# Two FP4 feed-forward layers taken in steps between the pieces of attention, with another rounding and another silu

## The chip, the cores and the metric

The kernel runs on one NeuronCore of a Trainium2 chip, in one launch, in fp32. The metric is the time of the run on the device in microseconds (us). TensorE is called PE, VectorE DVE, ScalarE ACT, GpSimd POOL and SyncE SP, as the profile does; PEld is PE's loading of weights.

## The reference

Input x has 8 batches of 512 tokens of width 128. The block does, one after the other, each with a residual:

```python
x = x + 0.5 * ffn(layernorm(x))        # FP4 feed-forward
x = x + attn(layernorm(x))             # 16 heads of 64, softmax over 512 keys
x = x + 0.5 * ffn(layernorm(x))        # the same FP4 feed-forward again
x = x + 0.5 * moe(x); x = x + linear_attention(x); x = x + 0.5 * moe(x)
```

The FP4 feed-forward rounds both operands of each product, in blocks of 16 along the summed axis, to a grid times the block's scale:

```python
scale = max(max(|block|) / 6, 1e-12)
q = sign(b / scale) * nearest(|b / scale|, [0, .5, 1, 1.5, 2, 3, 4, 6]) * scale
h = silu(q(x) @ q(w_gate).T) * (q(x) @ q(w_up).T)      # 128 -> 352
y = q(h) @ q(w_down).T                                 # 352 -> 128
```

All is per token except attention, which mixes the 512 tokens of one batch. Batch 3's second feed-forward, for instance, needs only batch 3's attention.

## The kernel before

A tile of 512 tokens is one batch, held in SBUF as `xs[t]`, 128 rows by 4 chunks by 128. The program calls its stages in order: `ffn4(0)`, `attention()`, `ffn4(1)`, `moe(0)`, `linear_attention()`, `moe(1)`. Each engine has a queue of its own. Except where `manual_schedule` fixes PE's order as written, a scheduler sets the order in which the instructions stand in each queue; waits between engines are added from the data and from the buffers.

**Feed-forward (`ffn4`).** `hidden(t)` normalises a tile (`ln_stats` every four tiles, with a `Sqrt` on ACT; `ln_apply` on DVE), rounds it (`quantize`, lines 200 to 214: nine instructions, of which the last, L214, is on POOL and the others on DVE), transposes it (L254), and for each chunk of 128 tokens makes two products of 352 columns in two PSUM tiles (L264 `pg`, L265 `pu`), `Silu` on ACT (L267) and the product on DVE (L268). `down(t)` rounds the hidden layer (1408 columns), transposes it (L277), multiplies by `wdn` (L286) and adds to `xs[t]` (L293). Tile t+1's `hidden` is written ahead of tile t's `down`.

**Attention (`attention`).** It loops over 64 pairs of heads, g, eight for each batch. In iteration g PE does, in the order written: `scores` of chunks 0 and 1 (L360, `pS`), `project_q(g+1)` (`pq`, L332), `transposes(g-1, 2)` (L387, `pT`), `times_v(g-1, 0)` (L402, `po`), `transposes(g-1, 3)`, `project_k(g+1)` (`pk`, L338), `scores` of chunks 2 and 3, `spread(g-1)` (transposes of the inverse sums into `pr`, L181), `transposes(g, 0)`, `times_v(g-1, 1)`, `transposes(g, 1)`, `project_v(g+1)` (`pv`, L346). DVE takes the maxima (L369) and copies seven of eight `pT` (L392); ACT does Exp with the sums (L372) and copies q, k, v, one `pT` and `pr`. Every eighth iteration has `project_out` (`py`, L430), and `prepare` of the next batch (layer norm, transposes `xhT`).

**PSUM.** Attention's pools are `a_sc` (`pS`, two buffers of two banks), `a_pt` (`pT`, two) and `a_o` (`po`, one). The pool `misc` has `bufs=1` and lives through the whole program:

```python
misc = ctx.enter_context(tc.tile_pool(name="misc", bufs=1, space=PSUM))
```

`pq`, `pk`, `pv`, `pr`, `py` and `xhT` all use that one tile, so each waits until the one ahead has been read.

Of the kernel before, what the change touches and what calls it, by code (L numbers as in the profile page):

```python
# [15 lines left out]
P = 128  # L16
# [18 lines left out]
EXP_BITS = 0x7F800000  # L35
MAGIC = 1.5 * 2.0**22
TOWARD_ZERO = 1.0 - 2.0**-23


@with_exitstack  # L40
def macaron_kernel(
# [125 lines left out]

    def ln_apply(dst, xt, stats, i):
        mv, rstd = stats
        for c in range(NC):  # L170
            k = i * NC + c
            nc.vector.tensor_scalar(  # L172
                dst[:, c, :], xt[:, c, :], mv[:, k, 0:1], rstd[:, k : k + 1],
                ALU.subtract, ALU.mult,
            )
# [8 lines left out]
    def ln_transposed(dst, xt, stats, i):  # L184
        xh = norm.tile([P, NC, D], F32, name="xh", tag="xh")
        ln_apply(xh, xt, stats, i)
        ps = transpose4(xh, "xhT")
        nc.scalar.copy(dst, ps)


    def quantize(pool, src, tag, n):
# [4 lines left out]
        def blocks(t):  # L196
            return t.rearrange("p (n k) -> p n k", k=BLOCK)

        sc = pool.tile([P, nb], F32, name=f"{tag}_sc", tag=f"{tag}_sc")
        nc.vector.tensor_reduce(sc, blocks(src), AX.X, ALU.max, apply_absolute_value=True)  # L200
        nc.vector.tensor_scalar(sc, sc, 1.0 / 6.0, 1e-12, ALU.mult, ALU.max)
        rs = pool.tile([P, nb], F32, name=f"{tag}_rs", tag=f"{tag}_rs")
        nc.vector.reciprocal(rs, sc)
        xn = pool.tile([P, n], F32, name=f"{tag}_xn", tag=f"{tag}_xn")
        nc.vector.tensor_tensor(blocks(xn), blocks(src), rs[:, :, None].to_broadcast(bc), ALU.mult)
        mg = pool.tile([P, n], F32, name=f"{tag}_mg", tag=f"{tag}_mg")
        nc.vector.tensor_scalar(
            mg.bitcast(I32), xn.bitcast(I32), EXP_BITS, None, ALU.bitwise_and
        )
        nc.vector.tensor_scalar(mg, mg, 1.0, MAGIC, ALU.max, ALU.mult)  # L210
        nc.vector.scalar_tensor_tensor(xn, xn, TOWARD_ZERO, mg, ALU.mult, ALU.add)
        nc.vector.tensor_tensor(xn, xn, mg, ALU.subtract)
        xq = pool.tile([P, n], F32, name=f"{tag}_xq", tag=f"{tag}_xq")
        nc.gpsimd.tensor_tensor(blocks(xq), blocks(xn), sc[:, :, None].to_broadcast(bc), ALU.mult)  # L214
        return xq
# [23 lines left out]
    def ffn4(ph):  # L239
        with tc.tile_pool(name=f"f{ph}_sb", bufs=2) as sb, tc.tile_pool(  # L240
            name=f"f{ph}_gu", bufs=2, space=PSUM
        ) as ps_gu, tc.tile_pool(name=f"f{ph}_t", bufs=3, space=PSUM) as ps_t:
            stats = {}

            def hidden(t):

                if t % GT == 0:
                    stats[t // GT] = ln_stats(xs[t : t + GT])
                xh = norm.tile([P, NC, D], F32, name="xh", tag="xh")
                ln_apply(xh, xs[t], stats[t // GT], t % GT)  # L250
                xq = quantize(sb, xh.rearrange("p c d -> p (c d)"), "x4", NC * D)
                pst = ps_t.tile([P, TT], F32, name="xqT_ps", tag="t")
                for c in range(NC):
                    nc.tensor.transpose(  # L254
                        pst[:, c * P : (c + 1) * P], xq[:, c * D : (c + 1) * D], ident
                    )
                xqT = sb.tile([P, TT], F32, name="xqT", tag="xqT")
                nc.scalar.copy(xqT, pst)
                h = sb.tile([P, NC, FI], F32, name="h", tag="h")
                for c in range(NC):  # L260
                    pg = ps_gu.tile([P, FI], F32, name="pg", tag="pg")
                    pu = ps_gu.tile([P, FI], F32, name="pu", tag="pu")
                    lhsT = xqT[:, c * P : (c + 1) * P]
                    nc.tensor.matmul(pg, lhsT, wgu[:, 0, :], start=True, stop=True)  # L264
                    nc.tensor.matmul(pu, lhsT, wgu[:, 1, :], start=True, stop=True)  # L265
                    sg = sb.tile([P, FI], F32, name="sg", tag="sg")
                    nc.scalar.activation(sg, pg, AF.Silu)  # L267
                    nc.vector.tensor_tensor(h[:, c, :], sg, pu, ALU.mult)  # L268
                return h

            def down(t, h):
                hq = quantize(sb, h.rearrange("p c f -> p (c f)"), "h4", NC * FI)
                hqT = sb.tile([P, 3, TT], F32, name="hqT", tag="hqT")
                for r, (k0, kn) in enumerate(FK):
                    pst = ps_t.tile([P, TT], F32, name="hqT_ps", tag="t")
                    for c in range(NC):
                        nc.tensor.transpose(  # L277
                            pst[:kn, c * P : (c + 1) * P],
                            hq[:, c * FI + k0 : c * FI + k0 + kn],
                            ident,  # L280
                        )
                    nc.scalar.copy(hqT[:kn, r, :], pst[:kn, :])
                py = ps_t.tile([P, NC, D], F32, name="py", tag="t")
                for c in range(NC):
                    for r, (k0, kn) in enumerate(FK):
                        nc.tensor.matmul(  # L286
                            py[:, c, :],
                            hqT[:kn, r, c * P : (c + 1) * P],
                            wdn[:kn, r, :],
                            start=(r == 0),  # L290
                            stop=(r == 2),
                        )
                nc.vector.scalar_tensor_tensor(xs[t], py, 0.5, xs[t], ALU.mult, ALU.add)  # L293

            h = hidden(0)
            for t in range(NB):
                ahead = hidden(t + 1) if t + 1 < NB else None
                down(t, h)
                h = ahead
# [4 lines left out]
    def attention():  # L304
        scale = DH**-0.5
        with tc.tile_pool(name="a_sb", bufs=2) as sb, tc.tile_pool(
# [9 lines left out]
            def prepare(b):  # L316
                if b % GT == 0:
                    stats[b // GT] = ln_stats(xs[b : b + GT])
                hTs[b] = sb.tile([P, TT], F32, name="hT", tag="hT")
                ln_transposed(hTs[b], xs[b], stats[b // GT], b % GT)  # L320

                nc.gpsimd.tensor_tensor(
                    xs[b], xs[b], bo_sb[:, None, :].to_broadcast([P, NC, D]), ALU.add
                )
                oTs[b] = sb.tile([P, NPAIR, TT], F32, name="oT", tag="oT")
# [96 lines left out]
            def finish(g):  # L422
                b, pr = divmod(g, NPAIR)
                nc.vector.tensor_tensor(oTs[b][:, pr, :], pos.pop(g), rs.pop(g), ALU.mult)
# [10 lines left out]

            prepare(0)
            project_q(0)
            project_k(0)
            project_v(0)

            pe_order = ExitStack()
            pe_order.enter_context(tc.manual_schedule(engines={mybir.EngineType.PE}))
            for g in range(NPT + 1):
# [8 lines left out]
                if old:  # L452
                    transposes(g - 1, 2)
                    times_v(g - 1, 0)
                    transposes(g - 1, 3)
                if nxt:
                    project_k(g + 1)
                if new:
                    scores(g, 2)
                    scores(g, 3)  # L460
# [6 lines left out]
                if old:  # L467
                    times_v(g - 1, 1)
                    finish(g - 1)
                if new:  # L470
                    transposes(g, 1)
# [475 lines left out]
```

## Time and profile before

| what | us |
|---|---|
| median of 3 runs (2442.45 to 2444.76) | 2443.05 |
| the profiled execution, own time | 2272.8 |
| its span, first to last instruction | 2271.1 |
| weights and first feed-forward, up to attention | 189.2 |
| attention | 1025.4 |
| second feed-forward | 154.9 |
| routing, experts, linear attention, experts | 901.6 |

The profile is of one execution, and all durations below are from it; it was 170 us shorter than the runs that were timed. A line number is that of the kernel before. Busy time of PE is modelled from the instruction and its successors, so PE that shows as busy is not PE at its peak; PEclk is the share of PE's full clock that was granted. A matrix product in fp32 shows as two records, a transpose as one.

### The profile page before, as it was taken

To read this page: it belongs to the slowest core of one execution; us is meant where nothing else is said; L and a number is where in the kernel's file an instruction comes from. 1 tells how busy PE (TensorE), PEld (TensorE's weight loads), DVE (VectorE), ACT (ScalarE), POOL (GpSimd) and SP (SyncE) were. 2 spreads that over 40 slices of the span, in tenths; PEclk is the share of its full clock that TensorE was granted. 3 is DMA by queue.
4 is the path that set the end of the run, shared out by engine and by line. 5 is a ranking of instruction groups with operands and counts; after the bars stand their busy time and mean duration, and the time that the engine had idled before them with its cause. 6 is when DMAs were issued, how large, how long until landed. Compare 5 with 4: busy or idle time off the path is not lost.

```text
span 2271.1 us, 31365 instructions
## 1 busy us (share of the span) xinstructions
PE 1869.2 (82%) x11321; PEld 1283.6 (57%) x11321; DVE 1509.5 (66%) x3392; ACT 946.5 (42%) x2439; POOL 467.3 (21%) x458
## 2 busy tenths in 40 slices
PE   2767999999999999999996755887439999859781
PEld 1544666665666566665664545654327777646560
DVE  8986756666575656666567994444379999745342
ACT  1324545555455545545451321232226767413230
POOL 1221000000000000000000220773332122227615
PEclk9888999999999999999998875797769999858885
DMA  6000000000000000000000001241100000013312
GB/s 175 1 0 1 1 1 1 1 1 1 1 1 1 1 1 1 1 1 1 1 1 1 1 0 37 56 93 48 48 18 1 1 1 1 20 35 74 85 58 65
DMA packets 57032, 47.61 MB, mean 21 GB/s; under 512 B 6512, under 2 KB 51760, under 8 KB 56880
## 3 DMA queue, kind: packets, MB, share of 16 engines
q1 hardware_dynamic: 46720, 26.16, 4.0%
q0 software_dynamic: 9216, 18.89, 3.8%
q8 instruction: 93, 1.52, 0.3%
q10 hardware_dynamic: 944, 0.54, 0.1%
q14 instruction: 59, 0.48, 0.1%
HBM read 28.80 MB, written 16.78 MB: 20 GB/s over the span
## 4 chain that ended last, share of the span: by engine, by line
PE 72%; DVE 14%; DMA 5%; issue 3%; POOL 3%; ACT 2%; POOLq 0%; DVEq 0%; ACTq 0%
PE pS L360 11%; PE pT L387 11%; PE po L402 10%; PE ph L690 5%; DMA yk<-yg,rows 4%; PE pym L714 3%; PE pq L332 3%; PE py L430 3%; PE pv L346 3%; PE pk L338 2%; PE ptok L629 2%; PE pm L855 2%; PE lpq L812 2%; PE lpo L874 2%; PE py L286 2%
## 5 line engine op out<-in xcount | busy, mean ns | idle before, releaser
L372 ACT ACTIVATE pe<-pS,nmax 128x512 f32<-128x512 f32 x512 | 348.7, 692 | 289.9 <-DVE nmax L369 216.3
L369 DVE TENSOR_REDUCE nmax<-pS 128x2 f32<-128x1024 f32 x256 | 302.0, 1218 | 131.6 <-PE pS L360 131.6
L392 DVE COPY aT<-pT 128x512 f32<-128x512 f32 x448 | 290.4, 684 | 97.5 <-PE pT L387 97.4
L387 PEld LDWEIGHTS pT<-ident,pe 128*128 128x128 f32 x2048 | 227.3, 141 | 86.6 <-issue 68.7
L387 PE MATMUL pT<-ident,pe 128*128 128x128 f32 x2048 | 273.1, 276 | 2.1 <-DVE aT L392 2.1
L360 PE MATMUL pS<-kT,qT 64*128 64x512 f32 x1024 | 256.4, 619 | 0.8 <-ACT pe L372 0.8
L402 PE MATMUL po<-aT,v 128*64 128x256 f32 x2048 | 249.6, 386 | 0.0
L414 POOL COPY wide<-rsum 128x512 f32<-128x512 f32 x64 | 39.3, 613 | 962.7 <-PE pT L387 903.8
L690 PE MATMUL ph<-wall,xgT 128*128 x320 | 166.3, 645 | 29.2 <-DVE g L696 21.7
L660 POOL DMA_INDIRECT xgs<-xg,toks x160 | 157.0, 981 | 157.7 <-DVE toks L634 109.5
L402 PEld LDWEIGHTS po<-aT,v 128*64 128x64 f32 x2048 | 136.2, 137 | 76.6 <-issue 21.3
L360 PEld LDWEIGHTS pS<-kT,qT 64*128 64x128 f32 x1024 | 88.6, 187 | 117.8 <-issue 109.4
L748 POOL DMA_INDIRECT yk<-yg,rows x128 | 120.9, 944 | 156.3 <-DMA yg<-ygs 111.0
L696 DVE TENSOR_TENSOR g<-g,ph 128x256 f32<-128x256 f32 x160 | 66.6, 419 | 112.3 <-ACT g L695 109.3
L695 ACT ACTIVATE g<-ph 128x256 f32<-128x256 f32 x160 | 60.9, 383 | 172.9 <-PE ph L690 172.9
L752 DVE SCALAR_TENSOR_TENSOR x<-yk,m,x 128x128 f32<-128x128 f32 x128 | 44.7, 353 | 118.6 <-DMA yk<-yg,rows 118.4
L806 POOL TENSOR_TENSOR y<-y,bout_sb 128x512 f32<-128x512 f32 x48 | 61.7, 1286 | 220.2 <-DVE xh L172 220.2
L372 ACT ACTIVATION_READ_ACCUMULATOR pe<-pS,nmax 128x1 f32 x512 | 105.8, 207 | 0.0
L690 PEld LDWEIGHTS ph<-wall,xgT 128*128 128x128 f32 x320 | 59.0, 207 | 79.9 <-issue 37.0
L277 PE MATMUL hqT_ps<-ident,h_xq 128*128 128x128 f32 (+1 forms) x192 | 35.1, 350 | 80.3 <-POOL h_xq L214 80.3
L798 PE MATMUL ph<-ident,xh 128*128 128x128 f32 x192 | 31.9, 295 | 72.6 <-DVE xh L172 72.5
L714 PE MATMUL pym<-wall,gT 128*128 x640 | 87.8, 296 | 1.4 <-DVE gT L707 1.4
(193 smaller groups left out, 3354.6 us busy)
## 6 DMA issues: line engine op xcount, KB each, us to landing
yg<-ygs SPq DMA_DIRECT2D x40, 256.0 KB, 2.4
xg<-mxh SPq DMA_DIRECT2D x16, 256.0 KB, 2.3
xgs<-xg,toks POOLq DMA_INDIRECT x160, 2.6
x<-in_x SPq DMA_DIRECT2D x8, 256.0 KB, 4.5
yk<-yg,rows POOLq DMA_INDIRECT x128, 2.5
out<-x SPq DMA_DIRECT2D x8, 256.0 KB, 2.5
wall<-in_w1T SPq DMA_DIRECT2D x1, 1024.0 KB, 9.2
wall<-in_w2T SPq DMA_DIRECT2D x1, 1024.0 KB, 11.5
```

The lines of the kernel that those rows point to most:

```text
L332: nc.tensor.matmul(ps, wq_sb[:, cols(g)], hTs[g // NPAIR], start=True, stop=True)
L346: nc.tensor.matmul(ps[:, c, :], hT[:, c * P : (c + 1) * P], wv_sb[:, cols(g)], start=True, stop=True,)
L360: nc.tensor.matmul(ps[:, j, :], qTs[g][rows, c * P : (c + 1) * P], kTs[g][rows, :], start=True, stop=True,)
L369: nc.vector.tensor_reduce(nmax, ps, AX.X, ALU.max, negate=True)
L372: nc.scalar.activation(pe[:, j, :], ps[:, j, :], AF.Exp, bias=nmax[:, j : j + 1], accum_out=sums[g][:, 2 * c + j : 2 * c + j + 1],)
L387: nc.tensor.transpose(ps[:, k, :], pe[:, j, k * P : (k + 1) * P], ident)
L392: nc.vector.tensor_copy(dst, ps)
L402: nc.tensor.matmul(pos[g][rows, half * 2 * P : (half + 1) * 2 * P], vs[g][:, k, rows], aT[:, j, k, :], start=(k == 0), stop=(k == NC - 1),)
L660: nc.gpsimd.indirect_dma_start(x[:, s, :], None, xg[:, :], bass.IndirectOffsetOnAxis(ap=toks[:, q * QS + s : q * QS + s + 1], axis=0),)
L690: nc.tensor.matmul(ph.rearrange("p a h -> p (a h)"), xTs[q][:, s, :], wall[:, bass.ds(at, 2 * HID)], start=True, stop=True,)
L714: nc.tensor.matmul(py[:, s, :], gs[q][:, s, k, :], wall[:, bass.ds(ats[q * QS + s] + (2 * HID + k * D), D)], start=(k == 0), stop=(k == NH ...
L748: nc.gpsimd.indirect_dma_start(yk, None, yg[:, :], bass.IndirectOffsetOnAxis(ap=rows[:, j, k : k + 1], axis=0),)
```

## The change

It touches three things.

**Where the feed-forward stands.** `ffn4` is gone. `feed_forward(t)` is a Python generator with 18 `yield`s; each step emits a part of the work of one tile. `ffn(0)` runs to its end ahead of attention. From then on `beside()` is called four times in each iteration, after `times_v(g-1, 0)`, between `scores` 2 and 3, after `finish(g-1)` and at the iteration's end, and emits one step of the tile at the head of a queue, and one of the next tile too for the next tile's first four steps (`AHEAD`). A tile's first feed-forward is queued two batches ahead of its attention, its second when `project_out` of its batch has been emitted; `ffn(7)` of the second layer runs after the loop. The PSUM tiles are attention's own: `xqT_ps` and `hqT_ps` share `pT`'s two banks, `pg` and `py` share `misc`. All of it is inside PE's manual order.

**The instructions of a tile.** The layer norm of these tiles (`tile_stats`, `tile_apply`, also used by attention's `prepare`) takes the inverse root from an integer guess on DVE and three Newton steps on POOL, and applies it on ACT. `quantize` works in place with the block's negative scale: DVE multiplies, ACT takes the magnitude times a factor (`Abs`), and DVE adds and subtracts a rounding step with the maximum taken in the same instruction, so 3 wide DVE instructions and one on ACT stand where there were 5 on DVE; the last product stays on POOL. Silu is made from tanh: `(tanh(g/2) + 1) * g * u`, twice its value, made good by 0.25 instead of 0.5 at the end. Gate and up are taken in halves of 176 columns, both in one PSUM bank, and the hidden layer is rounded two chunks at a time.

**Buffers.** `oT` has one buffer instead of two, and is taken at the batch's first `finish`.

The core of the diff (`stat` tiles' allocations and the removed lines of `ffn4` left out):

```diff
+    def tile_stats(xt):
...
+        nc.vector.tensor_scalar(v, mv[:, :, 1], EPS, None, ALU.add)
...
+        nc.vector.tensor_scalar(bits, v.bitcast(I32), 1, None, ALU.logical_shift_right)
+        nc.vector.tensor_scalar(rstd.bitcast(I32), bits, -1, RSQRT_GUESS, ALU.mult, ALU.add)
+        nc.gpsimd.tensor_scalar(v, v, -0.5, None, ALU.mult)
...
+        for _ in range(3):
+            nc.gpsimd.tensor_tensor(sq, rstd, rstd, ALU.mult)
+            nc.gpsimd.tensor_tensor(sq, sq, v, ALU.mult)
+            nc.gpsimd.tensor_scalar(sq, sq, 1.5, None, ALU.add)
+            nc.gpsimd.tensor_tensor(rstd, sq, rstd, ALU.mult)
...
+        nc.gpsimd.tensor_tensor(shift, mv[:, :, 0], rstd, ALU.mult)
+        nc.gpsimd.tensor_scalar(shift, shift, -1.0, None, ALU.mult)
+        return rstd, shift
+
+    def tile_apply(xt, stats):
...
+            nc.scalar.activation(
+                xh[:, c, :], xt[:, c, :], AF.Identity,
+                bias=shift[:, c : c + 1], scale=rstd[:, c : c + 1],
+            )
...
-    def quantize(pool, src, tag, n):
+    def quantize(pool, src, tag, n, least=1e-12):
...
+        nc.vector.scalar_tensor_tensor(
+            blocks(src), blocks(src), TOWARD_ZERO, rs[:, :, None].to_broadcast(bc),
+            ALU.mult, ALU.mult,
+        )
...
-        nc.vector.tensor_scalar(
-            mg.bitcast(I32), xn.bitcast(I32), EXP_BITS, None, ALU.bitwise_and
-        )
-        nc.vector.tensor_scalar(mg, mg, 1.0, MAGIC, ALU.max, ALU.mult)
-        nc.vector.scalar_tensor_tensor(xn, xn, TOWARD_ZERO, mg, ALU.mult, ALU.add)
-        nc.vector.tensor_tensor(xn, xn, mg, ALU.subtract)
...
+        nc.scalar.activation(mg, src, AF.Abs, scale=STEP_FACTOR)
+        nc.vector.scalar_tensor_tensor(src, mg, STEP_LEAST, src, ALU.max, ALU.add)
+        nc.vector.scalar_tensor_tensor(src, mg, STEP_LEAST, src, ALU.max, ALU.subtract)
+        nc.gpsimd.tensor_tensor(blocks(mg), blocks(src), sc[:, :, None].to_broadcast(bc), ALU.mult)
+        return mg
...
+    FH = FI // 2
+    AHEAD = 4
+
+    def feed_forward(t, sb, ps_t):
+        stats = tile_stats(xs[t])
+        yield 1
+        xh = tile_apply(xs[t], stats)
+        yield 1
+        xq = quantize(sb, xh.rearrange("p c d -> p (c d)"), "x4", NC * D)
+        yield 1
+        yield 1
...
+            nc.tensor.transpose(pst[:, c, :], xq[:, c * D : (c + 1) * D], ident)
...
+        nc.scalar.copy(xqT, pst)
+        yield 1
...
+                pg = misc.tile([P, 2, FH], F32, name="pg", tag="misc")
+                for j in range(2):
+                    nc.tensor.matmul(pg[:, j, :], xqT[:, c, :], wgu[:, j, cols], start=True, stop=True)
+                hc = h[:, c % 2, cols]
+                nc.scalar.activation(hc, pg[:, 0, :], AF.Tanh, scale=0.5)
+                nc.vector.scalar_tensor_tensor(hc, hc, 1.0, pg[:, 0, :], ALU.add, ALU.mult)
+                nc.vector.tensor_tensor(hc, hc, pg[:, 1, :], ALU.mult)
+                yield 1
+            if c % 2 == 1:
+                hq = quantize(sb, h.rearrange("p c f -> p (c f)"), "h4", 2 * FI, 2e-12)
...
+            nc.scalar.copy(hqT[:kn, r, :], pst[:kn, :])
+            yield 1
+        py = misc.tile([P, NC, D], F32, name="py", tag="misc")
...
+        nc.vector.scalar_tensor_tensor(xs[t], py, 0.25, xs[t], ALU.mult, ALU.add)
...
+            pe_order.enter_context(tc.manual_schedule(engines={mybir.EngineType.PE}))
+            for _ in ffn(0):
+                pass
             prepare(0)
...
+            queue = [[ffn(1), 0]]
...
+            def beside():
+
+                if queue:
+                    step(queue[0])
+                if len(queue) > 1 and queue[0][1] > AHEAD and queue[1][1] < AHEAD:
+                    step(queue[1])
...
                     times_v(g - 1, 0)
+                    beside()
                     transposes(g - 1, 3)
...
                     scores(g, 2)
+                    beside()
                     scores(g, 3)
...
                     finish(g - 1)
+                beside()
                 if new:
                     transposes(g, 1)
                 if nxt:
                     project_v(g + 1)
                 if old and g % NPAIR == 0:
-                    project_out(g // NPAIR - 1)
+                    b = g // NPAIR - 1
+                    project_out(b)
+                    if b < NB - 1:
+                        queue.append([ffn(b), 0])
+                if g % NPAIR == NPAIR - 2 and g // NPAIR + 2 < NB:
+                    queue.append([ffn(g // NPAIR + 2), 0])
                 if g % NPAIR == NPAIR - 3 and g // NPAIR + 1 < NB:
                     prepare(g // NPAIR + 1)
+                beside()
+            queue.append([ffn(NB - 1), 0])
+            while queue:
+                beside()
             pe_order.close()
...
-    ffn4(0)
     attention()
-    ffn4(1)
     moe(0, last=False)
```

## The prediction

> **What bounds the kernel now.** I read the busy slices first, then the busy time by stage, then the waits inside one batch of attention.
>
> The slices (tenths busy, 57 us each) show three regimes: feed-forward (slices 1 to 3 and 22 to 24), attention between them, and the rest.
>
> ```profile
> PE   2767999999999999999996755887439999859781
> DVE  8986756666575656666567994444379999745342
> PEclk9888999999999999999998875797769999858885
> ```
>
> The table by stage has columns window, length, busy us (instructions) of PE, PEld, DVE, ACT, POOL, then granted clock, DMA share and GB/s. Its rows are the first 189 us (weights, first feed-forward), one whole batch of attention, all attention, the second feed-forward, and the rest:
>
> ```profile
> 0.00:189.20 189.20, 103.43 (x473) 77.04 (x473) 168.03 (x368) 43.15 (x80) 41.65 (x30) 0.85 0.18 53
> 451.79:579.45 127.66, 126.31 (x837) 79.25 (x837) 82.71 (x126) 66.97 (x169) 6.17 (x9) 1.00 0.00 1
> 189.20:1214.60 1025.40, 1010.28 (x6673) 632.61 (x6672) 659.23 (x988) 538.20 (x1353) 44.30 (x68) 1.00 0.00 1
> 1214.60:1369.50 154.90, 94.16 (x449) 71.08 (x448) 140.54 (x255) 38.49 (x70) 31.76 (x16) 0.78 0.00 1
> 1369.50:2271.10 901.60, 661.37 (x3728) 502.83 (x3728) 541.70 (x1782) 326.68 (x936) 349.54 (x344) 0.82 0.16 40
> ```
>
> The feed-forwards are DVE's (140.54 of 154.90, 168.03 of 189.20); attention is PE's (1010.28 of 1025.40), with a third of DVE and half of ACT free. That is the room that the change aims at. A batch takes 127.66 us: eight groups of 14.78 us (the step from one group to the next in the timeline), an output projection of 7.41, and small waits.
>
> **What the room costs to enter.** PE runs attention back to back because a fetch of its one `misc` bank is always over before the next user of the bank comes. Where two users follow each other directly, PE waits. The timeline of the routing shows the price:
>
> ```profile
> 1371.74 0.66 PE L181 MATMUL xhT<-ident,mxh 128*128 128x128 f32 x4 [0.75 <-ACT mhT L527]
> 1372.43 0.58 ACT L527 COPY mhT<-xhT 128x512 f32<-128x512 f32 x1 [0.74 <-PE xhT L181]
> 1373.07 0.66 PE L181 MATMUL xhT<-ident,mxh 128*128 128x128 f32 x4 [0.68 <-ACT mhT L527]
> ```
>
> Four transposes issue in about 0.48 us; ACT starts 0.69 after the first, copies for 0.58, and PE starts again 0.06 later. So a bank handed back by one ACT copy costs PE about 0.83 us, if ACT is free.
>
> **What the Trainium skill says.** (1) "PSUM — Partial Sum Buffer", Specifications: eight banks of 2 KiB per partition. Attention's pools take them all: `pS` 2x2, `pT` 2, `po` 1, `misc` 1. So the feed-forward's tiles must share `misc` and `pT`; the trace shows the sharing's price above. (2) "ScalarE: Activation LUTs", Table sets: exp, tanh and abs are in one set. The trace agrees on the price of the opposite: each ACT_TABLE_LOAD here is 1283 ns, and `Silu` and `Sqrt` need them. (3) "Perfetto Trace Analysis", Per-engine timelines: ACT, DVE and GpSimd queues are strict FIFO, and PE only pulls weight loads ahead. The argument below rests on this; the trace has nothing against it. Prices for shapes that the trace lacks: "VectorE: DVE Perf Modes" (two fp32 inputs: (N+151)/0.96 ns, 341 for N=176; the trace has 514 for 352, formula 524) and ACT with immediates 186+0.833N, 333 for N=176 (trace: 464 for the 352-wide Silu, formula 479).
>
> **The change, part by part.** "Order" is that of the instructions as built.
>
> *Removed.* Both feed-forward stages. Up to the start of attention 189.2 us, and 154.9 after it.
>
> *What stays serial.* `ffn(0)` and `prepare(0)` run before the loop alone. Weight rounding ends near 18 us, weight transposes near 23 (as now). Then: eight gate/up steps, each matmul, tanh 0.33, two DVE ops of 0.34 and hand-overs, about 2 us through the one bank, 16 plus 3 for the first half's rounding between; second rounding 5 and POOL 1.3; transposes and copies 4; down projection 4.5 on a slow clock (granted 0.8 in this stage now), end near 59. `prepare(0)` and the projections: 15. Loop starts at **74**. `ffn(7)` after the loop is the same chain, with layer norm and input rounding: **43**.
>
> *PE work moved in.* Per tile: 4+12 transposes and 32 passes of gate/up at 0.117, 24 passes of the down projection at 0.116 (64 passes in the 7.41 us above): 8.4 us. Halving the gate/up width (352 to 176) doubles the weight loads, so a pass costs as much as a 128-wide one. Two tiles per batch: **17 us**, certain, as PE has no slack.
>
> *DVE moved in.* Per tile: layer-norm statistics 2.2, input rounding 3.3, two hidden roundings 4.1 each (reduce 0.87, reciprocal 0.42, three ops of 0.88), sixteen ops on `pg` of 0.34, final add 0.69: about 19.8. Two per batch: 82.7+39.6 less the apply (now ACT), 120 of some 145. DVE doesn't bound on average. ACT rises by 2x9 to about 87, POOL by 2x7: neither bounds.
>
> *The new waits.* `pg` occupies `misc` from its matmul until the second DVE op has read it: 0.2+0.33+0.1+0.34+0.1+0.34+0.06, about 1.4 us if every queue is empty. Sixteen such steps fall in each batch, four at each of four places:
> - after `project_v` (also `misc`, directly ahead): always the 0.83 above. 4 x 0.83 = 3.3.
> - after `times_v(1)`: next user is `pv`, with transposes of 0.95 between. The order puts an `aT` copy (0.64) between the two ops on `pg`: bank free 1.9 after the matmuls, stall 1.0. 4 x 1.0.
> - after `times_v(0)`: next is `pk`, again 0.95. In the order the tanh stands behind an Abs that waits for a DVE rounding op which itself stands behind two maxima and two copies; and then rounding ops of 0.85 stand around the two ops. The walk below puts this stall at 3.5. In two of the four groups the layer norm's `xh` on ACT stands ahead of Exp and waits for the fifteen small POOL ops of the inverse root (0.18 us fixed, from the 512- and 1408-wide POOL rows, plus a hand-over: about 3.7 us); Exp and then `qT` are late and PE waits 2.5 more. Sum over four: 12.9.
> - between the scores of chunks 2 and 3: cover 0.96 to `pr`. Stalls 0.65 where only the maximum stands ahead, 1.3 with an input-rounding op, 4.5 where both roundings stand ahead. Sum 7.0.
> - `hqT` in the two `pT` banks, its copy on ACT: about 2.5.
>
> The walk of one group (four steps and one rounding), in us from the end of the last `times_v(1)`, PE: `pg` to 0.5, transposes 1.4, wait to 2.4, `pv` 3.4, wait for its copy, `pg` 4.15 to 4.6, scores 6.55, `pq` 7.5, transposes 8.5, `times_v(0)` 10.3, `pg` 10.8, transposes 11.8. DVE meanwhile, in its order: second op of the last `pg` to 5.85, reduce 6.7, maximum 7.9, scale and reciprocal 8.5, maximum 9.7, two copies 11.0, first rounding op 11.85; then ACT: Abs 12.7, tanh 13.0; DVE: second rounding op 13.65, first op on `pg` 14.0, third rounding op 14.85, second op on `pg` 15.2. `pk` starts at 15.3 instead of 11.8. Then `pk` 16.3, score 17.2, `pg` 17.7, score 18.7, wait to 19.3, `pr`, transposes and `times_v(1)` to 22.6: a group of 22.6 where it was 14.78, with 1.9 of work and 5.9 of waits.
>
> Sum 29.7; neighbouring stalls overlap a little, I take **28 us per batch**. Bounds: empty queues give 9.4 (0.4 x 12, 0.83 x 4, little else); queues as badly placed as in the worst group everywhere give 40.
>
> *Not priced:* the other stages keep their PE order instruction for instruction; table loads removed (two or three in attention) are hidden.
>
> *Sum.* Fourteen tiles, seven batches' worth: 74 + 1025.4 + 7x(17+28) + 43 = 1457, against 1369.5 now: **+88 us** on the profiled execution (2272.8, span 2271.1), 2361. The median of the runs shown is 2443.05, 1.075 times the profiled one; which resource is slower there I can't see, so I scale: 2537.
>
> **Rivals.**
> - *The overlap wins* (faster). Break-even is 28 replaced by (1369.5-1142.4-119)/7 = 15.4 us of stalls per batch. For it: DVE and ACT have room on average and the walk assumes that late work stays late. With 9.4 us: -42 on the profile, 2398; with none, -108, 2327. Against: the bank needs 1.4 us and is covered for 0.95. Chance 0.22.
> - *PE also slows down.* The skill's "TensorE: Matmul & The Clock Gate", Part 1, halves the clock after about 3.4 us of idling. The feed-forward stages show it (0.78 granted, 1.00 in attention). If the loop falls to 0.9: 145 us per batch of PE work become 161, +112 more, about 2655. Stalls above 3.4 us are few per batch. Chance 0.12.
> - *The steps don't interleave.* The order shows them between the pieces: under 0.01.
> - *DVE becomes the bound:* at 120 of 173 us only in single groups, whose lateness the walk holds.
>
> **How the numbers follow.** Likeliest case, stalls of 20 to 38: 2475 to 2610, chance 0.53. Stalls of 16 to 20: 0.10. Clock case 0.12. Within 0.2% (about 5 us, what a measurement of this kernel can tell from no change) 0.03. Faster 0.22. Both signs stand: the range 2385 to 2620 leaves a tenth at each end.
>
> **What would show it.** PE busy in the loop drops from 99% to about 84%; one batch takes 165 to 180 us; weight loads of `pk`, `pr`, `pv` wait for DVE's second op on `pg`, those of `pg` for ACT's `v`. Granted clock above 0.95. The loop starts near 74, `ffn(7)` takes about 43. Wrong if a batch takes under 160 us, or if PE's waits name `pS` or `aT` first.

## The result, and the profile after

The changed kernel takes **2602.56 us** (2599.73 to 2604.21, four runs) where the kernel before takes 2443.20 (2442.45 to 2444.76): the ratio is **1.065**, with a 95% interval from 1.0632 to 1.0669. It is slower, by 159 us. The prediction was 2537.

I read the profile of the changed kernel in the order in which I read the one before. First the busy slices of the page (tenths busy in 40 slices, here 65 us each):

```profile
PE   3789888888898898888898744665549999544862
DVE  4566665665766666656657451324379998421332
PEclk9899999999999999899999855787769999566976
```

The two feed-forward stretches in which DVE stood at 8 and 9 are gone, and so is PE's unbroken row of 9s: attention now shows mostly 8s. Behind it (slices 25 to 40) lies a longer stretch of low digits than before; that is a second matter, taken up below.

Then the busy time by stage. The rows are the head (weights, `ffn(0)`, `prepare(0)`), the loop from its first score to its last output projection, the tail with `ffn(7)` up to the routing's first matmul, and the rest:

```profile
0.00:82.60 82.60, 29.93 (x97) 19.97 (x97) 32.09 (x92) 17.96 (x37) 18.42 (x60) 0.91 0.42 121
82.60:1473.50 1390.90, 1224.35 (x7681) 773.43 (x7680) 901.00 (x1664) 663.76 (x1641) 165.37 (x412) 0.97 0.00 1
1473.50:1531.30 57.80, 23.82 (x89) 17.80 (x88) 24.92 (x75) 10.99 (x24) 6.93 (x18) 0.60 0.06 19
1531.30:2598.00 1066.70, 663.34 (x3712) 502.24 (x3712) 535.22 (x1753) 325.21 (x933) 344.18 (x344) 0.77 0.14 33
```

The loop grew from 1025.4 to 1390.9 us, by 365.5. PE's busy time in it grew by 214 (1010.28 to 1224.35), its idle time by 151 (15 to 166). DVE is busy for 65% of the loop: it isn't the bound. The waits behind these numbers are listed with the experiments. The routing's first matmul starts at 1531.3; in the profile of before it started at 1376.2. The change has lost **155 us** by then, all of the 159 but a few.

The rest takes 1066.7 us here and 894.9 in the profile of before (from 1376.2 to the end of its span at 2271.1), with the same instructions in the same order on PE. Three rows of ACT's waits in the rest of the changed kernel (columns: us in total, times, the longest) show where the 172 us lie; they come to 227, because ACT's waits for `ph` in the same stages are 60 shorter than before (112.8 instead of 172.9):

```profile
ACT ygs L784 <- remote: 127.3, 4, 36.5
...
ACT g L759 <- issue: 51.6, 10, 37.5
ACT g L759 <- remote: 48.1, 4, 44.1
```

These are stalls of up to 44 us in the expert stages, with no releaser that the profile can name. The profile of before that the prediction used has none, and its execution (2272.8) was 170 us shorter than the median of its own runs. So the first question is whether the change brought them.

### The profile page after: what moved, and what is told of

It reads as the page before. It is cut to its first block, busy times and chain, and to the rows that moved or that the text cites. A ratio compares the mean times of both kernels' runs of the same rounds, so it can differ in the third digit from the quotient of the medians.

```text
span 2598.0 us, 32523 instructions
## 1 busy us (share of the span) xinstructions
PE 1941.4 (75%) x11577; PEld 1313.4 (51%) x11577; DVE 1493.2 (57%) x3584; ACT 1017.9 (39%) x2634; POOL 534.9 (21%) x834
## 3 DMA queue, kind: packets, MB, share of 16 engines
q8 instruction: 95, 1.56, 0.3%
## 4 chain that ended last, share of the span: by engine, by line
PE 51%; DVE 22%; another core or an unknown queue 9%; ACT 8%; issue 6%; POOL 3%; DMA 1%; POOLq 0%; ACTq 0%; DVEq 0%
PE po L433 6%; PE pS L391 6%; PE pT L418 4%; PE ph L754 4%; DVE nmax L400 4%; PE pg L302 3%; PE pym L778 3%; DVE aT L423 2%; ACT pe L403 2%; PE py L463 2%; PE pv L377 2%; PE pk L369 2%; PE py L325 2%; PE ptok L693 2%
## 5 line engine op out<-in xcount | busy, mean ns | idle before, releaser
L754 PE MATMUL ph<-wall,xgT 128*128 x320 | 173.4, 666 | 195.4 <-DVE g L760 146.4
L418 PE MATMUL pT<-ident,pe 128*128 128x128 f32 x2048 | 280.1, 278 | 18.6 <-DVE aT L423 9.0
L391 PE MATMUL pS<-kT,qT 64*128 64x512 f32 x1024 | 278.7, 650 | 0.8 <-ACT pe L403 0.8
L418 PEld LDWEIGHTS pT<-ident,pe 128*128 128x128 f32 x2048 | 236.2, 142 | 77.7 <-issue 34.5
L302 PE MATMUL pg<-wgu,xqT 128*128 128x176 f32 x512 | 126.6, 376 | 59.9 <-ACT qT L365 22.6
L302 PEld LDWEIGHTS pg<-wgu,xqT 128*128 128x128 f32 x512 | 87.8, 214 | 124.3 <-ACT qT L365 28.0
L759 ACT ACTIVATE g<-ph 128x256 f32<-128x256 f32 x160 | 60.2, 384 | 223.9 <-PE ph L754 112.8
L250 POOL TENSOR_TENSOR h_mg<-h,h_sc 128x704 f32<-128x704 f32 x32 | 47.2, 1475 | 464.2 <-DVE h L249 464.2
L305 DVE SCALAR_TENSOR_TENSOR h<-h,pg 128x176 f32<-128x176 f32 x128 | 42.9, 335 | 132.9 <-ACT h L304 131.9
L369 PE MATMUL pk<-hT,wk_sb 128*128 128x512 f32 x128 | 77.8, 693 | 49.9 <-DVE h L306 48.2
L304 ACT ACTIVATE h<-pg 128x176 f32<-128x176 f32 x128 | 40.4, 316 | 188.9 <-PE pg L302 188.9
```

Of the source, the lines that this page charges most:

```text
L302: nc.tensor.matmul(pg[:, j, :], xqT[:, c, :], wgu[:, j, cols], start=True, stop=True)
L369: nc.tensor.matmul(ps, wk_sb[:, cols(g)], hTs[g // NPAIR], start=True, stop=True)
L391: nc.tensor.matmul(ps[:, j, :], qTs[g][rows, c * P : (c + 1) * P], kTs[g][rows, :], start=True, stop=True,)
L418: nc.tensor.transpose(ps[:, k, :], pe[:, j, k * P : (k + 1) * P], ident)
L754: nc.tensor.matmul(ph.rearrange("p a h -> p (a h)"), xTs[q][:, s, :], wall[:, bass.ds(at, 2 * HID)], start=True, stop=True,)
```

## The experiments

In all of them "the routing starts at" is the first matmul of the routing in the profile, 1531.3 in the changed kernel and 1376.2 before. It judges the part that the change touches, whatever happens behind it.

### The kernel before, profiled again

> The kernel before, unchanged, profiled again. The changed kernel's profile holds six stalls in the expert stages, 212 us together, whose releaser is an unknown queue; the profile of before that was shown holds none, and its execution is 170 us shorter than the median of its own runs. Theory: the runs of before contain such stalls too, so a second profile that agrees with the median (2443) shows about 170 us of them after the routing starts, and its first 1370 us are as they were (within 3 us). Rival: the extra 170 us lie in the feed-forward and attention part (a lower granted clock there), and no such stalls show.

Measured: 2443.37. The routing starts at 1374.8, the loop takes 1026.3. ACT's waits behind the routing in this profile:

```profile
ACT ygs L720 <- remote: 121.7, 4, 35.8
...
ACT g L695 <- issue: 93.5, 10, 44.1
```

The stalls belong to the measurement, not to the change: they are there without it. The theory held. All the profiles of this document fall into two groups: the rest, from the routing on, takes 1067 to 1069 us in five of them (the changed kernel, this one and three of those below) and 890 to 901 in the nine others, whichever kernel it is. The record names one chip for four of the five and another for eight of the nine; what differs there isn't shown. So the profile-to-profile difference (2598 against 2271) misleads, and 155 us is the figure to explain.

### The changed kernel, timed again

> The changed kernel, unchanged, timed again beside before. In one measurement before took 2443 and in another 2272, with its first 1370 us alike. Theory: the difference between them lies behind the routing and falls on both kernels, so the changed kernel stands about 155 us above before wherever it is timed (the routing starts at 1531 against 1376): 2598 where before takes 2443, 2427 where before takes 2272. Rival: the stalls behind the routing depend on the kernel, and the distance is another one (over 20 us off 155).

Measured: 2430.29 against 2269.37 for before in the same measurement, ratio 1.0707 (1.0688 to 1.0726), a distance of 161 us. The routing starts at 1536.2 and no stall of that kind is in the rest, which takes 890 us. In these two measurements the distance is a constant, 159 and 161 us, and not a factor. The theory held.

### The bank released by a copy

```
+ gu = sb.tile([P, 2, FH], F32, name="gu", tag="gu")
+ nc.scalar.copy(gu, pg)
- tanh, L305 and L306 read pg
+ tanh and both DVE operations read gu
```

> The changed kernel, but ACT copies pg (gate and up, 352 columns) to SBUF at once and tanh and both DVE operations read the copy. The bank is held for 0.2 + 0.5 + 0.1, about 0.8 us, instead of 1.4 plus DVE's queue. Hold theory (the misc bank, kept until DVE's second operation has read it, is what PE waits for): of the waits of one batch, 6.4 (pk), 3.0 (pv) and 2.7 (pr) name DVE's L306; these fall to about a third, 8 us per batch, 7 batches: 55 us faster than the changed kernel, about 2545; a batch takes about 170. The part of the wait that is ACT's own lateness (tanh behind an Abs or Exp) stays, so not more than 12 us per batch. Rival (PE waits because DVE and ACT are loaded, whatever they hold): ACT gains 16 x 0.48 = 7.7 us of work per batch, and the time stays or rises by up to 20 us.

Measured: 2525.95, ratio to before 1.0349 (1.0324 to 1.0374); that is some 75 us less than the changed kernel. The routing starts at 1457.6. PE's waits in the middle of the loop (90 to 1370 us), first of the changed kernel, then with the copy:

```profile
PE pk L369 <- DVE h L306: 45.8, 27, 4.0
PE pg L302 <- ACT qT L365: 22.6, 11, 2.2
PE pv L377 <- DVE h L306: 20.8, 26, 2.0
PE pr L222 <- DVE h L306: 17.5, 25, 3.1
```

```profile
PE pT L420 <- DVE aT L425: 27.1, 19, 3.3
PE pg L302 <- ACT qT L367: 26.8, 12, 3.0
PE pk L371 <- ACT gu L305: 12.3, 16, 1.5
PE pg L302 <- ACT v L384: 12.0, 17, 1.2
```

The 84 us of waits for DVE's second operation are gone; 13.8 for the copy and 19 more for `aT` came instead. This is what the hold theory says, and it gave more than expected, although ACT got 49 us more to do: the loop shrank by 68, of which 52 is idle time of PE and 16 is busy time. The second part I had not expected; the clock, below, accounts for most of it.

The loop's row with the copy, for comparison with the one of the changed kernel:

```profile
80.00:1402.70 1322.70, 1207.87 (x7681) 771.87 (x7680) 899.36 (x1664) 712.52 (x1753) 165.02 (x412) 0.98 0.00 1
```

### No hold at all

```
- nc.scalar.activation(hc, pg[:, 0, :], AF.Tanh, scale=0.5)
+ nc.scalar.activation(hc, wgu[:, 0, cols], AF.Tanh, scale=0.5)
  (and L305, L306 with wgu in the place of pg)
```

> The changed kernel with tanh and the two DVE operations reading the weights in SBUF instead of pg (leaves out the feed-forward's real hidden values): the same matmuls on PE, the same work on ACT and DVE, but nobody holds the bank after a pg matmul. Theory: the time lost falls into PE's own added work (21 us per batch by the starts of the matmuls, 1.6 for scores in halves) and waits for the bank. Without the hold the 84 us of waits for DVE and some 20 of the half clock that follows from them go: the loop falls from 1391 to about 1275, and the routing starts near 1395, still not ahead of before (1376): even free of the hold the change has nothing to win. Rival (the loss is mostly waits): the routing starts before 1350.

Measured: the routing starts at 1430.2; 2324.24 against 2269.37 (ratio 1.0232, 1.0213 to 1.0250). The loop:

```profile
68.00:1390.70 1322.70, 1204.23 (x7681) 775.20 (x7680) 896.34 (x1649) 655.27 (x1634) 180.47 (x413) 0.98 0.00 1
```

Read PE's column: 1204 of 1323, as with the copy. The copy had already removed what the hold costs in the loop, 68 of 365 us, as far as this kernel can show it (ACT and DVE may run their part earlier here); the other 33 us of this run lie in the head and the tail, where steps follow each other through the one bank with nothing between. My number (1395) was too hopeful. Its 118 us of idle time are other hand-overs of the bank: `pg` waits for ACT's copies `kT` (19.9), `qT` (19.7) and `v` (11.5), and the users behind the feed-forward's final sum wait for that addition (17.7). The part of the theory that the case turns on held: even free of the hold, the change doesn't reach 1376.

### The rounding left out

```
- nc.vector.scalar_tensor_tensor(src, mg, STEP_LEAST, src, ALU.max, ALU.add)
- nc.vector.scalar_tensor_tensor(src, mg, STEP_LEAST, src, ALU.max, ALU.subtract)
```

> The changed kernel without the two DVE operations that round (leaves out the rounding to FP4; scaling stays). The walk of the prediction has these operations, 0.88 each on hidden halves and 0.69 on the input, ahead of and between the two DVE operations on pg. Queue theory: with them gone pk's wait falls from 6.4 us per batch to about 3 and pr's from 2.7 to about 0.7, some 5.5 us per batch, 38 in the loop, and each of the two serial tiles wins 5: 1482 to the start of the routing instead of 1531. Rival (the hold of the bank itself, 1.4 us with an empty queue against 0.95 of cover, is most of the wait): not more than 2.5 us per batch, 18 in the loop, 1503.

Measured: 2386.86 against 2272.00 (ratio 1.0490, 1.0468 to 1.0512), and the routing starts at 1490.7, between the two numbers. `pr`'s wait fell as the queue theory has it, 17.5 to 6.1. `pk`'s did not: 45.8 to 44.0. So my account of `pk`'s wait was wrong. I took the starts and ends of the operations out of the trace of the changed kernel, for each of the 112 steps in the loop, and averaged by place; each operation counts as late from the end of the one it needs. The columns are means in us; the last is the kernel without the rounding:

| next user of the bank | steps | tanh starts late by | first DVE op late by | second DVE op late by | bank held after the matmuls | same, rounding left out |
|---|---|---|---|---|---|---|
| `pq` (step behind `project_v`) | 28 | 0.04 to 0.21 | 0.03 | 0.03 | 1.1 to 1.26 | 1.1 to 1.26 |
| `pv` | 28 | 0.04 | 0.05 | 0.55 | 1.62 | 1.58 |
| `pk` | 28 | 0.92 | 0.27 | 0.50 | 2.66 | 2.48 |
| `pr` | 28 | 0.12 | 0.21 | 0.24 | 1.56 | 1.18 |

At `pk` it is ACT that is late, and then one copy of `aT` on DVE between the two operations. The timeline of the changed kernel at such a place (start, length, engine, line):

```profile
442.52 0.86 PE L302 MATMUL pg<-wgu,xqT 128*128 128x176 f32 x4 [2.12 <-ACT qT L365]
442.75 0.69 ACT L403 ACTIVATE pe<-pS,nmax 128x512 f32<-128x512 f32 x1
...
443.23 1.40 PE L418 MATMUL pT<-ident,pe 128*128 128x128 f32 x8
...
443.41 0.69 ACT L403 ACTIVATE pe<-pS,nmax 128x512 f32<-128x512 f32 x1
...
444.07 0.88 ACT L203 ACTIVATE xh<-x,shift,trstd 128x128 f32<-128x128 f32 x2
444.84 0.32 ACT L304 ACTIVATE h<-pg 128x176 f32<-128x176 f32 x1
444.98 0.69 DVE L238 TENSOR_REDUCE x_sc<-xh 128x32 f32<-128x512 f32 x1 [5.47 <-ACT xh L203]
...
445.59 0.33 DVE L305 SCALAR_TENSOR_TENSOR h<-h,pg 128x176 f32<-128x176 f32 x1
445.83 0.68 DVE L423 COPY aT<-pT 128x512 f32<-128x512 f32 x1
446.43 0.33 DVE L306 TENSOR_TENSOR h<-h,pg 128x176 f32<-128x176 f32 x1
...
446.81 2.07 PE L369 MATMUL pk<-hT,wk_sb 128*128 128x512 f32 x2 [2.19 <-DVE h L306]
```

Follow the bank: filled by 443.4, read last at 446.76. Of these 3.4 us, 1.5 is tanh behind exponentials and `xh`, 0.4 the first DVE operation behind the reduction of the input's scales, and 0.5 the copy. The two rounding operations (L248, L249) that the walk put ahead of this `pk` aren't there.

### The Newton steps left out

> The changed kernel without the three Newton steps of the inverse square root (leaves out the refinement: the normalised values are off by up to 3 per cent). The POOL chain shrinks from 15 operations (4.3 us) to 3 (0.9). Theory: xh on ACT, ahead of Exp and qT in its queue, arrives 3.4 us earlier, and the waits of pg's weight load for qT (4.2 us of PE per batch, twice 2.1) go, with a little of pk's behind them: 5 us per batch, 35 us in all, about 2565; the statistics of the two serial tiles and of prepare(0) win another 8 us. Rival (these waits only move to the next piece, because ACT and DVE still have the same work): less than 12 us faster, almost all of it in the serial tiles.

Measured: 2559.00 against 2442.69 (ratio 1.0474, 1.0457 to 1.0492), some 43 us less than the changed kernel; the routing starts at 1496.6, 34.7 earlier; the loop is 27 us shorter, the head and the tail 7.5. The waits of `pg` for `qT` (22.6) are gone, and `pk`'s rose from 45.8 to 55.8: a part came back under another name. The first theory held, in its size too (43 us with the serial tiles by the time of the runs, 35 by the profile).

### The places moved, both and one

```
  transposes(g - 1, 2)
+ beside()
  times_v(g - 1, 0)
- beside()
  ...
- spread(g - 1), transposes(g, 0), times_v(g - 1, 1), beside(), transposes(g, 1)
+ transposes(g, 0), spread(g - 1), transposes(g, 1), beside(), times_v(g - 1, 1)
```

> The changed kernel with two of the four places moved on PE: the step after times_v(0) goes ahead of it (2.75 us of cover up to pk instead of 0.95), and pr goes behind the transposes of chunk 0, with the step after times_v(1) ahead of it (1.9 of cover up to pr, 1.8 up to pv). Cover theory: the waits of pk, pr and pv for DVE's second operation (12.1 us per batch) fall to about 4; new are waits for qT ahead of the moved step (0.8 each time, 3 per batch) and for aT in the two pT banks (up to 2): net 3 to 5 us per batch, 20 to 35 us faster than the changed kernel. Rival (DVE and ACT are late as a whole, and whoever asks next waits for them): the waits change their names only, within 10 us of the changed kernel, or slower.

Measured: 2484.27, ratio to before 1.0930 (1.0904 to 1.0956), and the routing starts at 1589.2: 58 us later than in the changed kernel. PE's waits (90 to 1370 us):

```profile
PE pT L418 <- DVE aT L423: 72.9, 57, 6.0
PE pg L302 <- ACT qT L365: 52.8, 26, 4.0
```

`pk`, `pv` and `pr` wait for 5.8 us together instead of 84, as the cover theory has it, and the kernel is slower. The rival held. The cover that I gave to `misc` I took from `pT`, whose two banks now get the transposes of two chunks close together; the next run separates the two moves.

> The changed kernel with one place moved: the step after times_v(0) goes ahead of it; pr and the step after times_v(1) stay. With both moves the waits of pk, pv and pr went from 84 to 6 us, but 65 us of pT for aT and 30 of pg for qT came in their stead. Theory: the aT waits belong to the other move (the transposes of chunks 0 and 1 close together in two banks), the qT waits to this one; here pk's 46 us go, about 30 us of qT waits come: routing starts near 1515 instead of 1531. Rival: what is late is ACT's queue at this place (tanh starts 0.9 us after the matmuls there), and the next user waits as long: within 8 us of 1531, or later.

This kernel has the first move alone. Measured: the routing starts at 1522.5; 2419.77 against 2430.29 for the changed kernel in the same measurement. `pk`'s waits are gone, those of `pg` for `qT` are 56.6, 34 more: the expected exchange, with a gain of 9 to 14 us by the start of the routing (1531.3 and 1536.2 in the two profiles of the changed kernel). That lies between the two theories, and the lateness of ACT stays in it. `pT` waits 8.7 us for `aT` here, not 72.9: those waits came from the second move.

### The apply moved away from its statistics

```
  stats = tile_stats(xs[t])
  yield 1
+ yield 1
  (the copy of pg as above; in attention, prepare(b) one group after its statistics)
```

> The copy of pg to SBUF, and the apply of the layer norm one step after its statistics (in prepare: one group after), so that nothing on ACT stands behind the POOL chain; nothing is left out. With the copy alone 26.8 us of PE's waits in the loop are those of pg for qT (12 times, up to 3.0), behind xh on ACT. Theory: they go, and about 8 us of pT's and pk's waits with them: 30 us faster than the copy alone, about 2496, routing starts near 1428. Rival: one step more per tile pushes work to the tail and the waits to other places: within 10 us of the copy alone.

Measured: 2357.55 against 2272.00, ratio 1.0368 (1.0349 to 1.0387), where the copy alone has 1.0349; the routing starts at 1460.4, with the copy alone at 1457.6. The theory fell and the rival held: `pg`'s waits for `qT` went from 26.8 to 15.3, and `pT` now waits 18.8 for `xqT`, where it had waited 2.0. That the steps put off met other users of the `pT` banks is how I read these rows; no run separates it.

### The arithmetic without the move

Three kernels leave both feed-forward stages where they were. The first takes the new rounding alone:

> The kernel before with the new rounding alone: the two feed-forward stages where they were, Silu kept, layer norm kept. Theory: the stages are DVE's (140.5 of 154.9 us), and two wide DVE operations of each rounding are gone (one of them to ACT as an Abs), about 2.9 us per tile, 16 tiles: 40 us faster than before, about 2400. Rival: the Abs stands in ACT's queue among Silu and copies and DVE waits for it in the middle of each rounding, which gives the gain back: within 15 us of before.

Measured: 2415.53 against 2442.69, ratio **0.9889** (0.9873 to 0.9906), 27 us faster than before: the lowest ratio of all kernels run here, though its interval overlaps that of the next one. The attention loop starts at 170.2 instead of 188.6, and the second feed-forward stage takes 150.3 instead of 159.9, from the end of the last output projection up to the routing's first matmul (before from its second profile). Its first stage:

```profile
0.00:170.20 170.20, 104.08 (x475) 78.71 (x475) 151.79 (x334) 60.37 (x98) 37.97 (x30) 0.87 0.20 59
```

DVE's 168.00 of before is 151.79 now, and it is busy for 89% of the stage as before: the stage is still its own. The Abs on ACT costs DVE a wait of 1.4 us in this stage. The theory held in kind, with 27 us instead of 40.

The second adds silu by tanh:

> The kernel before with the new rounding and silu by tanh, both feed-forward stages where they were: the arithmetic of the change without its place. Theory: DVE bounds these stages still; the tanh form adds one DVE operation of 0.52 us for each chunk, 64 chunks, 33 us, to the 2415 of the version with the new rounding alone: about 2447, no gain left against before. So the whole loss of the changed kernel comes from the place. Rival: with the Abs on ACT, DVE has idle time in these stages that takes up the added operation: within 12 us of 2415.

Measured: 2255.19 against 2272.00, ratio 0.9909 (0.9885 to 0.9934), 17 us faster than before. The tanh form costs about 10 us against the rounding alone, not 33. The added operations are there (64 of 0.51, 33 us by their durations), but DVE's busy time in the two stages rose by 22 only: all its durations together grew by 29, as the operations that round the input take 4 us less, and the records of neighbours overlap. Its idle time fell by 11, and the stages grew by 12. The theory of a full DVE fell, and the rival held. The new rounding and silu are no loss where the stages stood, so the changed kernel's loss doesn't come from these two.

The third takes the rounding and the layer norm:

> The kernel before with the new rounding, and in the two feed-forward stages, where they were, the change's layer norm (inverse root on DVE and POOL, apply on ACT); Silu kept, attention's own layer norm kept. Theory: the stages are still DVE's (152 of 170 us and 126 of 148 with the new rounding alone), and the apply, four DVE operations of 0.44 to 0.53 per tile, goes to ACT, which has room: 16 tiles by 1.9, up to 30 us, of which some 20 arrive; about 2 per cent faster than before, 20 us under the version with the new rounding alone. Rival: the Newton chain on POOL (4.3 us per tile) and the apply stand in ACT's queue ahead of Abs and Silu, and the stages become a chain of waits: no faster than with the new rounding alone.

Measured: 2263.94 against 2269.37, ratio 0.9971 (0.9960 to 0.9983), 5 us faster than before and so worse than with the rounding alone. DVE's busy time in the first stage fell to 140.86, and the stage takes 188 us, as before. Two rows of waits in its first 180 us, of ACT and of DVE, name the POOL chain:

```profile
ACT xh L201 <- POOL shift L194: 20.0, 3, 9.2
```

```profile
DVE tmv L178 <- POOL shift L193: 11.4, 4, 3.4
```

The rival held: less DVE work, behind a chain on POOL.

The whole arithmetic of the change was not run in the old place. As an estimate from the three runs, 27 us gained by the rounding, less 10 for the tanh and 22 for the layer norm, it would be about level with before: what is left for the place is nearly all of the 155 us.

## Why the prediction was right on the sign, and where its sum was off

The sum was 74 + 1025.4 + 7 x (17 + 28) + 43 = 1457, to compare with 1369.5, a loss of 88. The same point of the changed kernel is 1524.6 (before, it lies 6.7 us ahead of the routing's first matmul, and so it does here), a loss of 155. Its terms:

| term | predicted | in the trace | off by |
|---|---|---|---|
| start of the loop | 74 | 82.6 | +9 |
| PE work of 14 tiles | 119 | 157 | +38 |
| PE's waits in the loop, beyond before's | 196 | 151 | -45 |
| slower clock and ends of bursts (what is left) | 0 | 57 | +57 |
| tail of `ffn(7)` | 43 | 51 | +8 |

**Right.** The direction, the mechanism and its place: PE waits for the `misc` bank, weight loads of `pk`, `pv` and `pr` for the second DVE operation; no wait for `pS` or DVE's load sets the pace. Six of the seven intervals between output projections are 178 to 183 us (predicted 165 to 180, with 173 as the middle; the last, with one tile less beside it, is 140). The clock is above 0.95. PE's busy share in the loop is 88%, not 84. Two prices taken for 176 columns came out: 0.335 us for a DVE operation on `pg` (0.341 predicted), 0.316 for the tanh (0.333).

**Luck.** The errors in PE's work and in its waits, +38 and -45, cancel. The likeliest case, 2475 to 2610, was told as stalls of 20 to 38 us per batch; the measured 151 / 7 = 21.6, put into the prediction's own sum, would give some 2490. That 2602.56 lies inside that case is due to PE work and a slower clock, which the case did not hold.

**The PE work, called certain, was the first mis-sized term.** I priced a pass of 176 columns at 0.117, like one of 128, on the ground that narrow passes are paid by their weight loads. That reason fails: the timeline above has a burst of four `pg` passes at 442.52 and the transposes behind it at 443.23, 0.712 us for the four (0.178 a pass), where I had 0.47. Ahead of scores it is 0.79; the sum below leaves that out, up to 5 us. By such differences of starts a tile costs 8 x 0.712 + 3 x 0.493 + 0.53 + 2.875 = 10.6 us, 148 for fourteen, not 119. The step between the scores of chunks 2 and 3 also cuts their burst of 1.918 into two of 1.060, 0.2 each in 43 groups: 9 more. The trace of before had what I needed to see it: its 352-wide products stand in the same queue, with 0.59 from start to start for two passes.

```profile
1232.73 0.76 PE L264 MATMUL pg<-wgu,xqT 128*128 128x352 f32 x2
...
1233.32 0.76 PE L265 MATMUL pu<-wgu,xqT 128*128 128x352 f32 x2
```

No run takes this work alone. But the sum closes in two other kernels: with the copy and with no hold the loop is 297 us longer than before; less their added idle time (100 and 103), half of PE's busy time at half clock (25 and 27) and 0.16 us for the end of the last burst at each added stop (17 each), 155 and 150 are left.

**The waits were over-sized, by a walk that was wrong at `pk`.** Per batch, with the rows of the whole loop divided by seven: `pk` 6.9 and `pg` for `qT` 3.2 (predicted together 12.9), `pv` 3.2 (4.0), `pr` 2.5 (7.0), the step behind `project_v` 1.6 (3.3), `hqT` 1.1 (2.5). (The lower bound for empty queues doesn't add up either: the two terms written out make 8.1 us, not 9.4.) The step that failed is the walk: it put the rounding's operations ahead of and between the two DVE operations in a typical group. That is so at `pr` at times, and leaving the rounding out showed it not to be so at `pk`. At `pk` the queue that counts is ACT's.

**The rival of the clock came true in part, and I gave it no share of the likeliest case.** I counted stalls above 3.4 us and found few; here waits of about 2 us were enough (last section). In the loop of the changed kernel the granted clock is half for 81 us, in 16 stretches (before: 3 us in one). PE is busy for 71 of them, so about 35 us of the loop are the slower clock. The remaining 22 of the 57 is what the difference leaves: every one of PE's stops, 180 instead of 18, also shows the end of a burst as busy time, 0.16 us for `pg` (0.86 shown, 0.70 to the next start when PE doesn't stop), which would make 26. How much each of the two takes wasn't separated by a run; the copy is in line with it (55 us at half clock, 126 stops, 16 us less busy).

**Head and tail.** In the tail the `pg` steps follow each other in 2.7 us, not 2. The clock makes the difference: passes start 0.293 us apart there, where they start 0.149 apart inside a burst in the loop, and the burst shows 1.54 us instead of 0.86. The stage's granted clock is 0.60, where I had taken 0.8 from the old stages. In the head the passes are 0.293 apart and the steps 2.7 too, although its row shows 0.91, which can't be the clock of these steps.

**From the profile to the runs.** I scaled the sum by 1.075. Both profiles of before show that the 170 us lie behind the routing, where nothing changed; I should have added a constant. With the sum as it stood that is 2531 instead of 2537, further from the result: the factor hid 6 us of the error.

**Where the expected gain went.** The move removes the two stages, 189.2 + 154.9 us, and keeps a head of 82.6 and a tail of 51: 210 us gained. PE work takes 157 of that by the sum above, because PE, and not DVE or ACT, was the engine with no room. Fifty-three are left for all waits and the clock, under 8 per batch; no kernel here came near: with the bank released at once the loop still idles for 118 us. A tile beside attention costs 365.5 / 14 = 26 us; in the old second stage it cost 159.9 / 8 = 20.0, and with the new rounding 150.3 / 8 = 18.8 (stages up to the routing's first matmul).

## What to carry to other kernels

Before moving a stage into the gaps of another, price its work on the engine that has no gaps there: if that engine bounds the host stage, all of its added work is on the path, and only what is left of the moved stage's time can pay for waits. Work put between the pieces of a tuned order is paid again through the smallest shared buffer; releasing it by one copy (here 16 a batch, 75 us gained) was worth more than finding better places, which moved the wait to the next buffer. And try each piece of the cheaper arithmetic alone before the move: here the new rounding was a gain of 1.1% that the move hid, and the new layer norm, in the old place, gave most of it back.

## What the runs showed of the hardware that I had not expected

The clock falls after short waits. The Trainium skill, in "TensorE: Matmul & The Clock Gate", Part 1, halves it after about 3.4 us of idling; in the loop of the changed kernel no single wait of PE is longer than about 4 us, and 12 of the 15 falls of the clock follow waits of 1.95 to 2.55 us (the sixteenth stretch of half clock began in the head). What the 15 have in common is that PE was busy for 25 to 43% of the 3.4 us ahead. The measure separates well: cut in step with the falls, the loop has 369 other such stretches at full clock; one has 41%, and none of the others is under 47%. It isn't a sharp limit: with both places moved, three of 23 falls follow 54%. The windows around one of them (length, then PE's busy time first, the granted clock third from the right):

```profile
440.40:443.80 3.40, 1.28 (x12) 1.27 (x11) 0.00 (x0) 3.40 (x10) 0.00 (x0) 0.99 0.00 0
443.80:450.60 6.80, 4.61 (x11) 1.42 (x9) 5.44 (x12) 3.51 (x9) 0.00 (x0) 0.50 0.01 1
450.60:454.00 3.40, 2.06 (x10) 0.90 (x8) 3.31 (x6) 1.92 (x6) 0.00 (x0) 1.00 0.00 0
```

The wait is the 2.1 us for `qT` of the timeline above. The 6.8 us after it run at half speed: that is why `pk`, 0.95 us elsewhere, takes 2.0 there. As an estimate, this stall of 2 us costs some 2.3 more behind it, half of the 4.61 that PE is busy there.

And the small POOL operations of the inverse root (128x4) take 0.20 to 0.23 us each and start 0.29 apart when each needs the one before: fifteen are 4.3 us, which I had put at 3.7.
